# Layer 1 of a hybrid network: where D u is computed, which engine adds a scan's steps, and how fine the convolution is scheduled

## The chip, the cores and the metric

The kernel runs on one core of a Trainium2 chip. A core has five engines with a queue of instructions each, taken in order: TensorE (PE, matrix products into PSUM), VectorE (DVE), ScalarE (ACT), GpSimd (POOL) and SyncE (SP, which here starts the DMA transfers). They meet through semaphores. The metric is the device time of one execution in microseconds; before the change the median of three runs is 7093.66 us.

## What is computed

The input is 16 images of 96 channels, 56 x 56, in float32. Four layers follow each other; only the second, layer 1, is touched by the change. It is a block with a selective scan (cut from the reference):

```python
u = _ln(z, norm1_g, norm1_b) @ in_proj_w.T                  # 96 -> Din = 192
uc = silu(conv_general_dilated(uc, conv_w, 'SAME', feature_group_count=Din))   # 3x3, nine taps
xs = stack([xf, xt, xf[..., ::-1], xt[..., ::-1]], axis=1)  # four directions
dt = softplus(einsum('bkrl,kdr->bkdl', dts, dt_projs_w) + dt_projs_b)
a = exp(dt * A)                                             # N = 1
bb = dt * Bs * xs
h = associative_scan(comb, (a, bb))                         # h = a h + bb along l
y = h * Cs + Ds * xs                                        # per direction
ym = _ln(y summed over the four directions); z = z + ym @ out_proj_w.T
z = z + fc2(gelu(fc1(_ln(z))))                              # 96 -> 384 -> 96
```

(`dts`, `Bs` and `Cs` are projections of `xs`; the parts that only reshape are left out.) The term D u is the same for all directions up to order, so the kernel uses the sum of the four D.

## The kernel before

Layer 1 keeps the 192 channels as one tile of 128 rows (`u0`) and one that holds the last 64 twice, once straight and once turned (`um`). Six combinations of channels and direction (i = 0 to 5) times two halves of the image are 12 *units*, and a unit has two parts of 784 positions: 24 *steps* per image, counted from 0 in the order i = 0, 3, 1, 4, 2, 5 (four steps each). The steps of i = 1 and 4 read u with rows and columns exchanged (turned).

A step on its engines:
- PE: p_d, two products that make dt's argument (L1237), queued in one stream with everything else that PE does.
- ACT: dt by an exponential (L1244) and a logarithm (L1246), then a by an exponential (L1253). The two a of a unit come after both its dt.
- SP: the rows B and C for the step, spread over the partitions by a DMA (bc, L1266).
- DVE: dt times u (L1325), times B into PSUM (L1328), the scan (L1334 forward, L1336 backward); and, one step late, hc = scan times C (L1289).
- The sum over directions: y lies in a tile of the pool `big`. For i = 0 and 2 (steps 0 to 3 and 16 to 19) DVE writes y = D u + hc (L1292, a scalar_tensor_tensor). For the other 16 steps POOL adds hc to y (L1358). hc has one buffer. After the last step DVE folds the turned half of the 64 channels into the straight one with four additions (L1363).

Around the scans of one image stand two more pieces, of its neighbours. The *front* of the next image: norm sums (p_s), input projection p_in (L1130), convolution p_c (L1170) as nine taps, each a diagonal product, in six blocks of 36 products by `convolved`, copies out of PSUM on ACT (L1191), two Silus (L1193), projection p_x (L1207), its copy (L1209) and the store of proj for the bc rows (L1213). The *back* of the image before: variance of y by squares (L1379, L1381) and p_v (L1387), `vr` on ACT and DVE (L1052, L1054), a root on POOL (L1404), then seven groups: p_o (L1417, L1418, L1425), z on DVE (L1428, L1432), squares (L1438), the variance (L1440 to L1443), a root on POOL (L1445), the product zn (L1447), a transpose p_t (L1451) and its copy (L1454), p_f and gelu (L1461, L1463), p_g (L1471, L1472) and z (L1474). The groups run as three chains; zn has one buffer, z and xr two.

The order of all this is not written out by hand. Each piece is a Python generator that yields an `Op` (engine, cost in us, buffers taken and given back) before the instructions it stands for. `in_order` picks, at every turn, the waiting piece with the smallest planned start plus a *lead* (a bias by engine and generator, table `TUNED`), and so fixes the order of each engine's queue when the program is built. An Op is one block: nothing can be put between its instructions. `hold` is added to an ACT piece that needs another table set. The lines of the planner and of the pieces that change:

```python
if op.engine == "ACT" and op.table and op.table != tables.get("ACT"):
    start, key = max(ready, engines.get("ACT", 0.0) + change["ACT"]), key + hold
...
if best is None or (start + key, rank) < best[:2]:
    best = (start + key, rank, i, start)
```

Seven tiles `big` serve u0, um and the two y of up to three images; y of the 64 channels gets the tile of u0 once its last step has read it.

Of the kernel before, what the change touches and what calls it, by code (L numbers as in the profile page):

```python
# [23 lines left out]
T = 448  # L24
# [35 lines left out]
def packed(x):  # L60
# [96 lines left out]
    for m in (C, DIN):  # L157
# [22 lines left out]
                        'zn': 1,  # L180
# [3 lines left out]
            'leads': {('PE', 'spreads'): -2.2,  # L184
                      ('PE', 'steps'): -3.4,
                      ('SP', 'sums'): -1.2,
                      ('ACT', 'spreads'): -0.3,
                      ('DVE', 'additions'): -0.2,
                      ('ACT', 'hidden'): -0.7,
                      ('SP', 'norms'): 0.7,  # L190
                      ('POOL', 'fronts'): -4.6,
                      ('DVE', 'some'): -0.3,
                      ('POOL', 'norms'): 0.4,
                      ('PE', 'some'): -0.6,
                      ('ACT', 'sums'): 0.5,
                      ('SP', 'projected'): -1.4,
                      ('DVE', 'norms'): 0.1,
                      ('POOL', 'backs'): -0.6,
# [3 lines left out]
                      ('ACT', 'fronts'): -0.2,  # L202
                      ('PE', 'fronts'): -2.4,
                      ('DVE', 'spreads'): -0.8,
                      ('SP', 'rows_of'): 0.2},
            'hold': 0.7,
# [52 lines left out]
def turned(ap):  # L259
    return ap.rearrange("c (h w) -> c w h", w=S)  # L260
# [626 lines left out]
def layer1(ctx, tc, src, given, dst, flags=None, soft=False):  # L887
# [151 lines left out]
    def pe(n, each, take=("ps",), give=(), **k):  # L1039
        return Op("PE", 1.05 * n * each, 0.25, take, give, **k)  # L1040
# [56 lines left out]
    def front(b, it):  # L1097
# [60 lines left out]
        def convolved(j):  # L1158

            pad, u = (whole, halves)[j], us[j]  # L1160
            for c in range(0, (8, 4)[j], 2):
                yield Op("none", 0.0, 0.0, take=("ps",))
                p = pair("p_c")
                yield pe(9, 0.66, ())
                for k in range(9):
                    for b in range(2):
                        r0 = 7 * (c + b) + k // 3
                        for s in range(2):
                            to = (s ^ b) * 64
                            nc.tensor.matmul(  # L1170
                                p[to : to + 64, b, :TC], taps[64 * s : 64 * s + 64, j, k],
                                pad[64 * s : 64 * s + 64, r0 : r0 + 7, k % 3 : k % 3 + S],
                                start=k == 0, stop=k == 8,
                            )
                at = TC * c
                if j == 0:
                    outs = [
                        (u[:, at : at + TC], p[:, 0, :TC], TC),
                        (u[:64, at + TC : at + 2 * TC], p[64:, 1, :TC], TC),
                        (u[64:, at + TC : at + 2 * TC], p[:64, 1, :TC], TC),  # L1180
                    ]
                else:
                    outs = []
                    for s, b in ((0, 0), (0, 1), (1, 0), (1, 1)):
                        to, row = (s ^ b) * 64, HALF_S * s + 7 * (c + b)
                        own = p[to : to + 64, b, :TC]
                        outs.append((u[:64, S * row : S * row + TC], own, TC))
                        outs.append((turned(u[64:])[:, row : row + 7], own.rearrange("p (h w) -> p h w", w=S), 1.7 * TC))
# [12 lines left out]
        for b in range(2):  # L1201
            yield pe(3, 0.7, ("ps",) if b == 0 else ())
# [17 lines left out]
    def made_of(it):  # L1220
# [4 lines left out]
        def steps():  # L1225

            for unit in units:
                i, h = unit
                order = (0, 1) if i < 3 else (1, 0)
                for s in order:  # L1230
# [11 lines left out]
                    else:  # L1242
                        yield act(SUB, give=("ps",), table="exp")
                        nc.scalar.activation(flat, p[:, :, :TC], AF.Exp, bias=dtb[:, i : i + 1])  # L1244
                        yield act(SUB, table="exp")
# [4 lines left out]
                for s in order:  # L1250
                    give = ("proj",) if last and s == order[1] else ()
                    yield act(SUB, give=give, table="exp", post=times[unit, s])
# [21 lines left out]
    def scanned(it):  # L1274
# [4 lines left out]
        def scan():  # L1279
            y0, ym = None, None  # L1280
            before, late = None, None

            def finish(unit, s, a, t, end, out, own_u):
                i = unit[0]
                yield dve(
                    SUB, take=("hc",), give=("bc",) + (("a",) if end else ()), post=None if i in (0, 2) else added[unit, s]
                )
                made[unit]["hc", s] = hc = buf([P, SUB], "hc")
                nc.vector.tensor_tensor(hc, a, t[:, 1], ALU.mult)  # L1289
                if i in (0, 2):  # L1290
                    yield dve(SUB, give=("hc",), post=added[unit, s])
                    nc.vector.scalar_tensor_tensor(  # L1292
                        out, own_u, dsum[:, i // 2 : i // 2 + 1], hc, ALU.mult, ALU.add
                    )

            for unit in units:
# [4 lines left out]
                if unit in ((0, 0), (2, 0)):  # L1301
                    yield Op("none", 0.0, 0.0, take=("big",))
                    y = big.pop(0)
                    if mixed:
                        ym = y
                    else:
                        y0 = y
                    it["y"].append(y)
                y = ym if mixed else y0
                for s in ((1, 0) if back else (0, 1)):  # L1310
# [10 lines left out]
                    yield dve(SUB, 1.85e-3 if flip else 1.04e-3, wait=times[unit, s], give=("big",) if free else ())  # L1321
                    if free:
                        big.append(u)
                    dt, a = made[unit][s], made[unit]["a"][:, SUB * s : SUB * s + SUB]
                    nc.vector.tensor_tensor(as_own(dt), as_own(dt), own(u), ALU.mult)  # L1325
                    yield dve(SUB, wait=bct[unit, s], give=("dt",))
# [11 lines left out]
                    late = (unit, s, a, t, end, own(y), own(u))  # L1338
            yield from finish(*late)

        def sums():
            for unit in units:
                i, h = unit
                back = i >= 3
                if i in (0, 2):
                    continue
                for s in ((1, 0) if back else (0, 1)):
                    at = HALF * h + SUB * s
                    yield Op("none", 0.0, 0.0, wait=added[unit, s])
                    y, u = it["y"][i == 5], (um if i == 5 else u0)  # L1350
# [6 lines left out]
                    yield Op("POOL", 1.9, give=("hc",))  # L1357
# [6 lines left out]

        it["sums"] = sums()
        yield from scan()

    def back(b, it):
# [38 lines left out]
        def group(g):  # L1407
# [18 lines left out]
            yield dve(4 * C1, take=("z",))  # L1426
# [17 lines left out]
            yield Op("POOL", 1.4)  # L1444
# [13 lines left out]
            def hidden(j):  # L1458
# [3 lines left out]
                yield act(T, table="gelu", give=("ps",))  # L1462
# [23 lines left out]
    def item():  # L1486
# [3 lines left out]
            "times": lists(), "bcs": lists(), "bct": lists(), "added": lists(),  # L1490
# [473 lines left out]
```

## Time and profile before

| | us |
|---|---|
| median of three runs (lowest, highest) | 7093.66 (7093.59, 7100.32) |
| the profiled execution | 7093.59 |
| its span, first to last instruction | 7091.7 |
| layer 1 within it, about | 1,146 to 4,402 |
| first scan, last scan of layer 1 | 1293 to 4288 |
| busy PE / DVE / ACT / POOL over the span | 6092.5 / 5440.8 / 4521.6 / 1377.5 |
| TensorE clock granted, mean | 0.904 |

Busy times of an engine count overlapping instructions once. The three layers on either side of layer 1 are one program with it, but do not overlap it: its scans lie in slices 8 to 24 of the page's 40. An instruction is given with the line of the kernel that issued it; "[7.13 <-ACT a L1253]" means that its engine stood idle for 7.13 us before it and that the last semaphore it waited for came from that line. PE's ends are modelled.

The costliest groups of layer 1 on the page are, per instruction: L1325 1304 ns, L1328 1010, L1289 968, the scans 1825, the additions L1358 2064, L1244 912, L1246 946, L1253 937.

### The profile page before, as it was taken

The page shows a single profiled execution, that of the slowest core. Times are in us where ns is not written, and L with a number is a line of the kernel's source. Part 1 is how long each engine was busy: PE and PEld are TensorE (multiplying, and loading weights), DVE is VectorE, ACT ScalarE, POOL GpSimd, SP SyncE. Part 2 cuts the span into 40 slices and gives each one's busy share as a digit, 9 for nine tenths or more (in the row PEclk, how much of TensorE's full clock was granted, in tenths as well). Part 3 has the DMA queues.
Part 4 walks back from the last instruction along what each step waited for, and adds up shares of the span by engine and source line. Part 5 has one row for each costly group of instructions (what it writes and reads, how often), then busy time and mean ns, then how long its engine had stood idle before and what let it go on. Part 6 is the DMA issues. An engine that isn't in the chain of part 4 may idle for free. (4 is left out here: it accounts for less than half of the span.)

```text
span 7091.7 us, 113066 instructions
## 1 busy us (share of the span) xinstructions
PE 6092.5 (86%) x45643; PEld 4183.4 (59%) x45643; DVE 5440.8 (77%) x7075; ACT 4521.6 (64%) x5897; POOL 1377.5 (19%) x898
## 2 busy tenths in 40 slices
PE   7999997888888888888888866788999989999986
PEld 3444443345445455555544444787888888888875
DVE  6786884598888888888888894667777777777775
ACT  4454542677777777777777762455666666666664
POOL 0000000233332323233332231111111111111110
PEclk9999997788898898888888867899999999999997
DMA  1111111444444444444544342445555455555542
GB/s 38 32 38 34 38 33 52 132 143 134 131 137 132 136 133 138 130 138 135 140 131 126 110 128 64 97 107 123 130 116 128 111 130 119 123 134 118 120 105 62
DMA packets 508374, 763.72 MB, mean 108 GB/s; under 512 B 206337, under 2 KB 339137, under 8 KB 504530
## 3 DMA queue, kind: packets, MB, share of 16 engines
q1 hardware_dynamic: 506818, 753.53, 41.2%
q8 instruction: 363, 5.95, 0.4%
q0 software_dynamic: 1024, 2.85, 0.1%
q14 instruction: 169, 1.38, 0.1%
HBM read 563.65 MB, written 192.59 MB: 107 GB/s over the span
## 5 line engine op out<-in xcount | busy, mean ns | idle before, releaser
L1664 POOL TENSOR_TENSOR r<-v,nhalf 112x16 f32<-112x16 f32 (+1 forms) x128 | 392.9, 3076 | 2238.8 <-DVE v L1662 1677.2
L1358 POOL TENSOR_TENSOR big<-big,hc 128x784 f32<-128x784 f32 x256 | 528.3, 2064 | 1139.4 <-DVE hc L1289 1131.3
L1325 DVE TENSOR_TENSOR dt<-dt,big 128x784 f32<-128x784 f32 x384 | 500.6, 1304 | 249.4 <-ACT a L1253 249.1
L827 DVE SCALAR_TENSOR_TENSOR h<-pad,rows,h 128x1568 f32<-128x1568 f32 x288 | 525.9, 1844 | 3.9
L1244 ACT ACTIVATE dt<-p_d,l_dtb 128x784 f32<-128x784 f32 x384 | 350.3, 912 | 183.0 <-PE p_d L1237 157.8
L1237 PE MATMUL p_d<-proj,l_dt 32*128 32x392 f32 x1536 | 382.8, 581 | 93.5 <-ACT big L1191 52.4
L1461 PE MATMUL p_f<-zt,w_fc 96*128 96x448 f32 x672 | 401.7, 731 | 41.9 <-ACT zt L1454 27.8
L1471 PE MATMUL p_g<-l_fc,hid 128*112 128x96 f32 x2688 | 425.5, 304 | 11.7 <-ACT hid L1463 11.0
L1722 PE MATMUL p<-k_f,z 112*128 112x112 f32 x3072 | 375.0, 282 | 67.5 <-DMA z<-d 57.9
L1722 PEld LDWEIGHTS p<-k_f,z 112*128 112x128 f32 x3072 | 370.6, 199 | 76.3 <-issue 57.9
L1471 PEld LDWEIGHTS p_g<-l_fc,hid 128*112 128x112 f32 x2688 | 385.4, 219 | 41.0 <-ACT hid L1463 30.8
L1770 PE MATMUL p_v<-w,gg 128*112 128x97 f32 x2048 | 377.9, 267 | 34.5 <-DVE gg L1759 11.6
L1170 PE MATMUL p_c<-x,taps 64*64 64x392 f32 x4608 | 400.8, 497 | 0.8 <-ACT big L1191 0.8
L1328 DVE TENSOR_TENSOR drive<-dt,bc 128x784 f32<-128x784 f32 x384 | 387.8, 1010 | 10.2
L1771 PE MATMUL p_v<-w2both,gg 128*112 128x97 f32 x2048 | 376.0, 266 | 0.0
L1289 DVE TENSOR_TENSOR hc<-a,bc 128x784 f32<-128x784 f32 x384 | 371.8, 968 | 3.4 <-POOL big L1358 3.4
L1246 ACT ACTIVATE dt<-dt,one 128x784 f32<-128x784 f32 x384 | 363.4, 946 | 8.5
L1691 PE MATMUL p_a<-first,xt 97*112 97x192 f32 x1792 | 336.6, 336 | 18.1 <-ACT xt L1685 9.0
L1334 DVE TENSOR_TENSOR_SCAN a<-a,drive 128x784 f32<-128x784 f32 x192 | 350.3, 1825 | 0.0
L1336 DVE TENSOR_TENSOR_SCAN a<-a,drive 128x784 f32<-128x784 f32 x192 | 350.2, 1824 | 0.0
L1253 ACT ACTIVATE a<-dt,aneg 128x784 f32<-128x784 f32 x384 | 347.5, 937 | 2.7 <-DVE a L1334 1.4
L800 PE MATMUL p_c<-pad,taps 64*64 64x392 f32 x4032 | 347.4, 494 | 0.3 <-ACT pad L782 0.3
(341 smaller groups left out, 14838.7 us busy)
## 6 DMA issues: line engine op xcount, KB each, us to landing
bc<-bc SPq DMA_DIRECT2D x256, 784.0 KB
bc<-bc SPq DMA_DIRECT2D x256, 392.0 KB
d<-y SPq DMA_DIRECT2D x448, 192.0 KB
z<-d SPq DMA_DIRECT2D x128, 672.0 KB
d<-uu SPq DMA_DIRECT2D x256, 169.8 KB
z<-d SPq DMA_DIRECT2D x192, 194.0 KB
xc<-x SPq DMA_DIRECT2D x96, 336.0 KB
x<-in_x SPq DMA_DIRECT2D x16, 1176.0 KB
```

Source lines behind the costliest of these rows:

```text
L827: nc.vector.scalar_tensor_tensor(out, view, taps9[:, i : i + 1], out, ALU.mult, ALU.add)
L1170: nc.tensor.matmul(p[to : to + 64, b, :TC], taps[64 * s : 64 * s + 64, j, k], pad[64 * s : 64 * s + 64, r0 : r0 + 7, k % 3 : k % 3 + S], s ...
L1237: nc.tensor.matmul(p[:, b, :TC], wdt[on, i], proj[on, h], start=True, stop=True)
L1325: nc.vector.tensor_tensor(as_own(dt), as_own(dt), own(u), ALU.mult)
L1328: nc.vector.tensor_tensor(b, dt, t[:, 0], ALU.mult)
L1358: nc.gpsimd.tensor_tensor(out, out, hc, ALU.add)
L1461: nc.tensor.matmul(p[:, 0, :T], w_fc1[:, P * j : P * j + P], zt, start=True, stop=True)
L1471: nc.tensor.matmul(p[:Q, q, :C], hid[:, j, own], fc2[:, j], start=j == 0, stop=False)
L1664: nc.gpsimd.tensor_tensor(r, v, nhalf[:, :n], ALU.pow)
L1722: nc.tensor.matmul(p[:, q, :Q], flat[:, P * (3 * q + k) : P * (3 * q + k) + P], f2, start=True, stop=True)
L1770: nc.tensor.matmul(out, gs[2 * h][:, at + k], w["w2"][:, 2 * h], start=True, stop=False)
L1771: nc.tensor.matmul(out, gs[1][:, at + k], w["w2both"][:, h], start=False, stop=True)
```

## The change

Layer 1 alone is changed, in four ways.

- y begins as D u. A new generator `inits`, beside the scan, lets ACT write y = (sum of D) times u, for each half of both tiles: four instructions of 1568 positions per image. The scalar_tensor_tensor on DVE is gone, and POOL adds hc in all 24 steps. A count `uses` frees u0 and um when both the scan and `inits` have read them.
- The nine taps of a convolution block are three Ops of three taps (12 products) in place of one of nine.
- zn has two buffers.
- Costs, leads and `hold` of the planner have other values, and some leads are new or gone.

```diff
@@ TUNED
-                        'zn': 1,
+                        'zn': 2,
-            'leads': {('PE', 'spreads'): -2.2,
+            'leads': {('PE', 'spreads'): -0.9,
-                      ('SP', 'sums'): -1.2,
+                      ('SP', 'sums'): 1.2,
-                      ('POOL', 'fronts'): -4.6,
+                      ('POOL', 'fronts'): -6.6,
-                      ('DVE', 'norms'): 0.1,
-                      ('POOL', 'backs'): -0.6,
+                      ('DVE', 'norms'): 1.5,
-                      ('PE', 'fronts'): -2.4,
+                      ('SP', 'some'): 4.2,
+                      ('ACT', 'inits'): 0.7,
+                      ('PE', 'hidden'): -1.2,
...
-            'hold': 0.7,
+            'hold': 0.0,
@@ estimates
-        return Op("PE", 1.05 * n * each, 0.25, take, give, **k)
+        return Op("PE", 1.1 * n * each, 0.25, take, give, **k)
...
@@ convolved
-                yield pe(9, 0.66, ())
                 for k in range(9):
+                    if k % 3 == 0:
+                        yield pe(3, 0.66, ())
                     for b in range(2):
@@ scan
-            def finish(unit, s, a, t, end, out, own_u):
+            def finish(unit, s, a, t, end):
...
                 nc.vector.tensor_tensor(hc, a, t[:, 1], ALU.mult)
-                if i in (0, 2):
-                    yield dve(SUB, give=("hc",), post=added[unit, s])
-                    nc.vector.scalar_tensor_tensor(
-                        out, own_u, dsum[:, i // 2 : i // 2 + 1], hc, ALU.mult, ALU.add
-                    )
...
+                    if free:
+                        it["uses"][mixed] -= 1
+                        if it["uses"][mixed] == 0:
+                            big.append(u)
+                            yield Op("none", 0.0, 0.0, give=("big",))
@@ sums
-                if i in (0, 2):
-                    continue
...
+                    yield Op("none", 0.0, 0.0, wait=it["begins"][i in (2, 5), h])
-                    yield Op("POOL", 1.9, give=("hc",))
+                    yield Op("POOL", 2.1, give=("hc",))
                     nc.gpsimd.tensor_tensor(out, out, hc, ALU.add)
@@ new
+        def inits():
+            for j, u in enumerate((u0, um)):
+                if j:
+                    yield Op("none", 0.0, 0.0, wait=added[(4, 1), 1])
+                yield Op("none", 0.0, 0.0, take=("big",))
+                y = big.pop(0)
+                it["y"].append(y)
+                for h in range(2):
+                    yield act(HALF, post=it["begins"][j, h])
+                    cols = slice(HALF * h, HALF * h + HALF)
+                    nc.scalar.activation(y[:, cols], u[:, cols], AF.Identity, scale=dsum[:, j : j + 1])
+                it["uses"][j] -= 1
+                if it["uses"][j] == 0:
+                    big.append(u)
+                    yield Op("none", 0.0, 0.0, give=("big",))
+
         it["sums"] = sums()
-        yield from scan()
+        yield [scan(), inits()]
```

## The prediction

> **What bounds the kernel now.** I read the slices of the page first: they show three stages, and only layer 1 (about 1,146 to 4,402 us) is touched. Then I read the busy times in windows over one image of its steady part, from the end of one image's four L1363 additions (2404.4) to the end of the next (2594.6), then the waits by engine, then the timeline at the longest waits. Columns of the windows: length; busy us (and count) of PE, weight loads, DVE, ACT, POOL; granted TensorE clock, DMA share, GB/s.
>
> ```profile
> 2404.40:2594.60 190.20, 163.64 (x1261) 93.93 (x1257) 163.00 (x179) 145.96 (x184) 58.78 (x40) 0.88 0.47 135
> ...
> 2424.20:2454.60 30.40, 23.96 (x281) 10.89 (x277) 20.34 (x22) 27.38 (x34) 5.33 (x3) 0.94 0.32 111
> 2454.60:2484.00 29.40, 23.97 (x159) 12.08 (x158) 18.47 (x27) 19.10 (x26) 14.40 (x16) 0.73 0.45 141
> 2484.00:2594.60 110.60, 99.00 (x631) 63.56 (x629) 105.30 (x114) 82.83 (x101) 39.05 (x22) 0.90 0.53 144
> ```
>
> A step is one of an image's 24 scans, counted from 0. An image takes 190.2 us; PE and DVE are busy 164 and 163 of them, so neither is the bound alone. The two middle rows (steps 4 to 7, and 8 with most of 9) hold 10.1 + 10.9 = 21.0 of DVE's 27.2 idle us; in the last row DVE is busy 95%. So the image has two regimes: while the next image's convolution runs, DVE waits; in the rest DVE is the bound. DVE's first row of waits (releaser; us in total, times, longest; 1,400 to 4,200 us) says for what, and the timeline (start, us, engine, line) shows an image's two longest, each as PE's queue and then DVE's step:
>
> ```profile
> DVE dt L1325 <- ACT a L1253: 223.3, 50, 10.8
> ```
> ```profile
> 2418.95 6.84 PE L1170 MATMUL p_c<-half,taps 64*64 64x392 f32 x72
> 2425.72 0.93 PE L1237 MATMUL p_d<-proj,l_dt 32*128 32x392 f32 x4
> ```
> ```profile
> 2431.45 0.97 DVE L1325 TENSOR_TENSOR dt<-dt,big 128x784 f32<-128x784 f32 x1 [7.13 <-ACT a L1253]
> ```
> ```profile
> 2454.47 6.69 PE L1207 MATMUL p_x<-big,l_xw 128*32 128x392 f32 x48 [2.62 <-ACT big L1193]
> 2461.09 0.93 PE L1237 MATMUL p_d<-proj,l_dt 32*128 32x392 f32 x4
> ```
> ```profile
> 2464.83 1.65 DVE L1325 TENSOR_TENSOR dt<-dt,big 128x784 f32<-128x784 f32 x1 [8.91 <-ACT a L1253]
> ```
>
> Both have one form: the small p_d matmul that feeds the next exponentials stands in PE's queue behind a block of 6.8 us (a whole nine-tap convolution, then the whole projection p_x), and DVE's step waits for the chain p_d, dt, a behind it.
>
> [...] the zn product L1447 takes 0.55 us alone and 2.57 under a GpSimd addition:
>
> ```profile
> 2314.81 2.57 DVE L1447 TENSOR_TENSOR zn<-z,r 112x384 f32<-112x384 f32 x1 [0.41 <-POOL r L1445]
> ...
> 2322.73 0.55 DVE L1447 TENSOR_TENSOR zn<-z,r 112x384 f32<-112x384 f32 x1
> ```
> ```profile
> 2314.74 2.23 POOL L1358 TENSOR_TENSOR big<-big,hc 128x784 f32<-128x784 f32 x1
> ```
>
> The scan [...] keeps 1.8 us beside additions. [...] the trace agrees (3136 elements 2.82, 784 elements 0.94: 0.80 ns), so D u over 1568 costs 0.94 + 784 x 0.80 ns = 1.57 us. [...] in the built order of layer 1 the loads are 242 before and 244 after.
>
> **The change part by part,** per image, by the order of instructions of both builds and the durations above.
> (1) The eight L1292 leave DVE. From hc to the scan it is 2366.26 to 2368.22 with one, 2390.35 to 2391.23 without: 1.96 - 0.89 = 1.07 each, 8.6 us. Four stand in steps 1 to 4, before a wait, four in steps 17 to 20, where DVE is the bound.
> (2) ACT gains 4 x 1.57 = 6.3 us (146 to 152 of the span). One stands among the exponentials of steps 0 and 1, one ahead of those of steps 2 and 3, two in a row (3.1 us) before those of step 18; queued behind these is a of step 18, which L1325 waits for. ACT may run ahead of DVE by three steps (three dt), so I take 1.5 us lost here (bounds 0 and 3.1). The second pair waits for a free big, which is u0 after step 15; ACT gets there later than that, cost 0.
> (3) POOL gains 8 additions of 1.85 us (a straight L1358; 2.23 is a turned one): 59 to 74 us. Each starts with the scan, which it doesn't block, and ends some 0.1 us into the next L1325 (1.08 against 0.97): 0.8 us. hc has one buffer; the next hc comes 4.5 us later at least, so the wait is 0 except after the 4.81 us root L1404, which now stands just ahead of step 4's addition: up to 0.9, under another wait.
> (4) zn products behind hc: before, by starts and ends in the trace, 59 of 112 ran into an addition, 3.7 per image at 1.92 against 0.55, 1.37 more; in the new order two per image stand right behind hc (steps 12, 21), 3.6 in all against 5.1: gain 1.5. The four L1363 now come right behind the last hc, not two instructions later, and wait about 2 us for its addition, against 1.54 that L1328 lost before (2.52 at 2395.28 against 0.98): loss 0.5. (3) and (4) cancel.
> (5) Taps in blocks of 12 matmuls (2.05 us). The built PE order uses it: 12 taps between three p_v groups, 24 then a p_v group, 12 before p_d. Steps 2 to 9 followed by hand on the three queues: p_d of step 4 still has three p_v groups and 36 taps ahead (about 11 us), yet p_d of step 3 comes earlier, and the wait at step 4 falls from 7.1 (6.0 on average) to 1 to 3. Gain 4.
> (6) p_x moves behind p_d of step 9 (before, it stood ahead of it), so a of step 8 needs the two Silus, not p_x. Chain: table 1.28 + Silus 5.64 + two squares 1.05 + variance 0.33 + table 1.28 + dt 1.85 + a 0.93 = 12.4 us, of which DVE fills about 8 with the second zn group (zn has two buffers now). The wait of 8.9 (with others in step 8: 10.0) becomes 3 to 5. p_x then lies under steps 8 and 9. Gain 5.5.
> (7) New lumps: between a of step 1 and a of step 2 ACT has some 18 us (four p_v preparations, nine copies, D u), which steps 0 and 1 with L1363 cover to about 1 us; step 20's exponentials follow two rounds of gelu and come 2 to 3 us late. Loss 2 more.
> SP: the built order has ten bc loads before the four proj stores (nine before), and proj is stored under step 9; bc of step 10 is then in time: 0. The other edits (estimates, hold, leads) act only through this order.
> Sum: 8.6 - 1.5 + 4 + 5.5 - 2 = 14.6, an image of about 175.6 us. There DVE would be busy 153 to 154, idle 22. My hand-followed queues close at 173; the difference is what such a count leaves out.
> Thirteen images run at the full pitch (L1363 comes every 188 to 191 us; its first and last intervals are 180 and 176, one is 194): 13 x 14.6 = 190. The first two and the last lack a back or a front: about 8.6 each, 26. The tail of the last back, where zn had one buffer: 0 to 5, taken 2. In all 218. The profiled span is 7091.7, its run 7093.59, 0.07 from the median: 7093.6 - 218 = **6876 us**.
>
> **Rivals.** (A) The waits only move: DVE's idle 27 us per image stays and just the 8.6 of DVE work goes. For: PE is busy 164 and has as much work as before. Against: 21 us of idle hang on two named blocks. 13 x 8.6 + 26 = 138: 6956. (B) Convolution steps gain nothing (PE is the bound there, four of the L1292 lie before a wait), only 4.3 in steps 17 to 20: 13 x 4.3 + 15 = 71: 7023. (C) More: fewer gaps also raise the granted clock (0.73 in the row of the p_x wait, 0.94 before it), p_d and gelu matmuls shorten, the pitch is 170: 13 x 20 + 30 = 290: 6804. (D) Slower: ACT becomes the bound through its order. The 18 us between a of steps 1 and 2 is not covered if p_v, one ysq buffer at a time, waits for PE's tap blocks: each of four rounds then costs about 2 us more, 8; the 3.1 of D u at step 18 and 3.4 at step 20 show fully, 2 at L1363: 16.5 of new waits against 8.6 gained, and (5) and (6) do not come: 13 x 8 = 104, about 7198. It decides when new waits pass 18 us per image. Against: ACT is busy 77% and ahead by up to three steps.
>
> **How the numbers follow.** Likeliest 0.50 (6820 to 6930), A 0.19, B 0.08, C 0.15, D 0.06, and 0.02 for no net effect. Pitches of 168 to 185 give 6780 to 7010; below lies a third of C (0.05), above D and part of B (0.11). 0.2% is 14 us, about what a measurement tells from no change. Faster 0.92, within 0.02, slower 0.06.
>
> **What would show it.** Right: pitch of L1363 near 176 us; L1325's wait for a down from 223 to about 100 in layer 1; DVE busy near 154 per image; no p_x between p_d and a of steps 8 and 9; POOL near 1,377 + 128 x 1.85 = 1,614 us. Wrong: ACT waits in L1325 at steps 2, 18 or 20 of over 4 us each; additions waiting for D u; hc waiting for POOL over 1 us per image; zn products near 2.5 us more often than now.

## The result, and the profile after

The changed kernel takes 7056.81 us (median of five runs, 7036.49 to 7063.0), the kernel before 7100.32 in the same session (7093.59 to 7112.2). The ratio is 0.9934, 95% interval 0.9915 to 0.9953: about 44 us faster, where 218 were forecast; 7056.8 lies 47 us above the upper end of the range. Layer 1 itself became 46.6 us shorter (it ends at 4355.6 us of the span, before at 4402.2). The untouched layers behind it took 9 us longer in this one profile, so its span fell by only 37.5, to 7054.2.

The same cut of the trace as before, windows over one image of the steady part: the whole image from the last L1352 (the old L1363) to the next, then its convolution steps (about 1 to 10), then the rest. Columns as in the prediction: length; busy us (and count) of PE, weight loads, DVE, ACT, POOL; granted TensorE clock, DMA share, GB/s. The changed kernel, then the same two parts of an image in the kernel before:

```profile
2397.78:2585.47 187.69, 166.82 (x1265) 94.70 (x1263) 152.56 (x170) 151.68 (x188) 73.16 (x48) 0.87 0.47 137
2397.78:2481.38 83.60, 74.72 (x750) 37.83 (x749) 60.39 (x69) 75.13 (x98) 27.85 (x23) 0.94 0.36 118
2481.38:2585.47 104.09, 92.10 (x517) 56.87 (x516) 92.17 (x103) 76.55 (x91) 45.31 (x26) 0.82 0.56 152
```
```profile
2404.44:2491.00 86.56, 71.61 (x670) 36.16 (x666) 63.30 (x70) 68.71 (x89) 21.11 (x20) 0.84 0.35 113
2491.00:2594.87 103.87, 92.27 (x594) 57.97 (x594) 99.94 (x110) 77.24 (x95) 37.67 (x21) 0.92 0.56 152
```

DVE is busy 152.6 us per image, as forecast (153 to 154). But the image takes 187.7 us and not 176: DVE now stands idle for 35.1 of it, before for 27.2. What left DVE came back as waiting. In the convolution steps ACT and PE are now busy for 90% of the time (75.1 and 74.7 of 83.6; before 79 and 83%), DVE for 72%. The rest of the image is no shorter than before (104.1 us against 103.9), although DVE has 7.8 us less to do in it: its idle time there rose from 3.9 to 11.9 us.

What DVE waits for, in the waits by engine (releaser; us in total, times, longest; 1,400 to 4,200 us). The changed kernel, then two lines of the kernel before:

```profile
DVE z L1479 <- PE p_g L1477: 156.5, 62, 6.0
DVE dt L1310 <- ACT a L1257: 128.2, 58, 4.7
DVE vr L1057 <- ACT vr L1055: 98.3, 51, 4.0
DVE big L1352 <- POOL big L1347: 27.4, 14, 2.0
```
```profile
DVE z L1474 <- PE p_g L1472: 74.1, 50, 3.8
DVE vr L1054 <- ACT vr L1052: 35.6, 52, 3.3
```

The wait for a (223.3 before) fell to 128.2, where about 100 was forecast, and no single one reaches 5 us. But z behind the gelu products rose from 74.1 to 156.5, vr from 35.6 to 98.3, and the first of the four L1352 of an image waits 2.0 us for GpSimd's last addition.

By step (busy and idle time between the ends of successive scans, my mean over the fourth to the fourteenth image of each trace), DVE's idle time moved as follows:

| step | 0 | 2 | 4 | 6 | 8 | 10 | 18 | 19 | 20 | all 24 |
|---|---|---|---|---|---|---|---|---|---|---|
| before | 0.7 | 0.5 | 6.0 | 1.1 | 10.0 | 1.6 | 2.6 | 0.1 | 0.1 | 27.4 |
| after | 4.5 | 7.2 | 4.7 | 4.5 | 3.2 | 2.9 | 0.0 | 2.1 | 2.3 | 35.6 |

By what ended it, the new idle time of step 0 is 2.3 us for p_g and 2.0 at the first L1352, that of step 6 is for vr and a, that of steps 19 and 20 for p_g.

Step 2 has the largest wait of the changed kernel. Its timeline (start, us, engine, line; in brackets the idle time ahead) shows DVE's queue and ACT's beside it:

```profile
2408.18 0.36 DVE L1057 SCALAR_TENSOR_TENSOR vr<-vr,p_v 128x196 f32<-128x196 f32 x1 [1.69 <-ACT vr L1055]
2412.57 0.36 DVE L1057 SCALAR_TENSOR_TENSOR vr<-vr,p_v 128x196 f32<-128x196 f32 x1 [4.03 <-ACT vr L1055]
2414.80 0.97 DVE L1310 TENSOR_TENSOR dt<-dt,big 128x784 f32<-128x784 f32 x1 [1.88 <-ACT a L1257]
```
```profile
2409.43 0.95 ACT L1250 ACTIVATE dt<-dt,one 128x784 f32<-128x784 f32 x1
2410.41 0.89 ACT L1195 COPY big<-p_c 64x392 f32<-64x392 f32 x1
2411.32 0.86 ACT L1384 ACTIVATE ysq<-big 128x784 f32<-128x784 f32 x1
2412.20 0.33 ACT L1055 ACTIVATE vr<-p_v 128x196 f32<-128x196 f32 x1
2412.56 0.85 ACT L1386 ACTIVATE big<-big 64x784 f32<-64x784 f32 x1
2413.44 0.48 ACT L1195 COPY big<-p_c 64x392 f32<-64x392 f32 x1
2413.82 0.95 ACT L1257 ACTIVATE a<-dt,aneg 128x784 f32<-128x784 f32 x1
```

Between the logarithm of dt and the a that uses it, ACT runs copies and a round of squares without a gap, 3.4 us of it; DVE meanwhile stands before vr, and then before a. D u is no part of this: its last instruction ahead of step 2 ends at 2395.96, and ACT then waits 1.88 us for p_d. Step 4 then waits 4.65 us, for another reason: its a is made once both p_d of its unit are done. On PE the first of them comes 14 us behind the p_d ahead of it, with three p_v rounds, taps and norm sums in between, and the second, on which ACT waits for 4.1 us, after three more blocks of three taps (x24 each, since the trace has two records for each product):

```profile
2403.30 0.93 PE L1241 MATMUL p_d<-proj,l_dt 32*128 32x392 f32 x4
...
2418.23 0.93 PE L1241 MATMUL p_d<-proj,l_dt 32*128 32x392 f32 x4 [0.53 <-ACT big L1195]
2419.72 2.21 PE L1174 MATMUL p_c<-half,taps 64*64 64x392 f32 x24 [0.56 <-ACT big L1195]
2421.74 2.16 PE L1174 MATMUL p_c<-x,taps 64*64 64x392 f32 x24
2423.72 2.16 PE L1174 MATMUL p_c<-half,taps 64*64 64x392 f32 x24
2425.81 0.93 PE L1241 MATMUL p_d<-proj,l_dt 32*128 32x392 f32 x4
```

Of the 46.6 us of layer 1, the eleven intervals in the middle (190.46 on average before, 188.22 after) give 25, the last three (558.7 before, 526.1 after) 32.6; the stretch from the last L1352 to the end of the layer gives 8.7 back, the start about 2.

### The profile page after: what moved, and what is told of

Read it like the earlier page. It is cut to its first block, busy times and chain, and to the rows that moved or that the text cites. A ratio compares the mean times of both kernels' runs of the same rounds, so it can differ in the third digit from the quotient of the medians.

```text
span 7054.2 us, 113146 instructions
## 1 busy us (share of the span) xinstructions
PE 6135.4 (87%) x45643; PEld 4203.5 (60%) x45643; DVE 5268.4 (75%) x6947; ACT 4618.1 (65%) x5963; POOL 1598.2 (23%) x1026
## 5 line engine op out<-in xcount | busy, mean ns | idle before, releaser
L1347 POOL TENSOR_TENSOR big<-big,hc 128x784 f32<-128x784 f32 x384 | 764.2, 1990 | 1539.5 <-DVE hc L1290 1493.0
L1174 PE MATMUL p_c<-x,taps 64*64 64x392 f32 x4608 | 429.9, 504 | 1.6 <-ACT big L1195 1.4
L1775 PE MATMUL p_v<-w,gg 128*112 128x97 f32 x2048 | 378.5, 267 | 33.5 <-DVE gg L1764 11.4
L1466 PE MATMUL p_f<-zt,w_fc 96*128 96x448 f32 x672 | 364.2, 687 | 22.3 <-ACT zt L1459 15.6
```

What stands on the lines that cost most here:

```text
L1174: nc.tensor.matmul(p[to : to + 64, b, :TC], taps[64 * s : 64 * s + 64, j, k], pad[64 * s : 64 * s + 64, r0 : r0 + 7, k % 3 : k % 3 + S], s ...
L1347: nc.gpsimd.tensor_tensor(out, out, hc, ALU.add)
L1775: nc.tensor.matmul(out, gs[2 * h][:, at + k], w["w2"][:, 2 * h], start=True, stop=False)
```

## The experiments

Times are medians; "ratio" is that to the kernel before in the same session, with its 95% interval. "Pitch" is the mean of eleven middle intervals of the image sums (L1363 or its successor) in the profiled run: 190.5 before, 188.2 after.

### 1. What one engine's work is worth, the order held fixed

My first theory on seeing the two traces was Q: PE's queue, busy for 90% of the convolution steps, is what they now wait for. Its rival V is the prediction's own accounting, in which DVE ends each step. The first cuts take away DVE's eight multiply-adds, about the same amount of DVE work in the changed kernel, and two thirds of the taps in both. The edits, with nothing else moved, are below; stt16_before, and later ln16_stt16_before and du16_after, also fill the big tiles once ahead of the first scan (18.6 us on POOL), so for these three the pitch says more than the time:

```diff
-  out, own_u, dsum[:, i // 2 : i // 2 + 1], hc, ALU.mult, ALU.add
+  out[:, :16], own_u[:, :16], dsum[:, i // 2 : i // 2 + 1], hc[:, :16], ALU.mult, ALU.add
```
```diff
+  n = 16 if i in (0, 2) else None
-  nc.vector.tensor_tensor(as_own(dt), as_own(dt), own(u), ALU.mult)
+  nc.vector.tensor_tensor(as_own(dt)[:, :n], as_own(dt)[:, :n], own(u)[:, :n], ALU.mult)
```
```diff
   for s in range(2):
+      if k % 4:
+          continue
```

> The kernel before with the eight multiply-adds of an image (L1292) cut to 16 of their 784 columns, so most of y in these steps is left out; its order of work is untouched, only a fill of the seven big tiles ahead of layer 1 is new (once, under 30 us). VectorE loses about 8 x 0.9 = 7.2 us per image. Theory Q (the chain through the scans runs over TensorE and ScalarE for more than half of the time, and these eight stand on it for only some 2.2 of their 8.6 us per image): pitch of the image sums 190.3 to 187.5-189.5, time 10 to 40 us less. Rival V (term 1 of the prediction: VectorE ends every step, its time counts in full): pitch 183 to 184, time about 90 to 105 us less.

> The changed kernel with the multiplication of dt by u (L1310) cut to 16 of 784 columns in the eight scans of an image over directions 0 and 2, so most of that product is left out; order untouched. VectorE loses about 8 x 0.85 = 6.8 us per image, as much as the change took from it. Theory Q (TensorE's queue is what the convolution steps wait for): pitch 187.7 to 185.5-187.7, time 0 to 35 us less. Rival V (VectorE still ends each step and the gain was lost to a worse order): pitch 181 to 182, time 80 to 100 us less.

> The kernel before with three of the nine convolution taps issued, so two thirds of layer 1's depthwise convolution are left out; order untouched. TensorE loses about 25 us per image in the steps 0 to 10. Theory Q: TensorE is on the chain there, but less than in the changed kernel: pitch 190.3 to 180-186, time 60 to 150 us less. Rival V: VectorE ends each step, only its waits for p_d's followers at steps 4 and 8 (16 us per image) can go: also 174 to 186; the two kernels gain alike.

> The changed kernel with three of the nine convolution taps issued, so two thirds of layer 1's depthwise convolution are left out; order untouched. TensorE loses about 25 us per image in the steps 0 to 10, where it is busy for some 95 per cent of the time. Theory Q (TensorE's queue is the bound in these steps): pitch 187.7 to 165-176, time 160 to 300 us less, clearly more than in the kernel before, and VectorE's waits at steps 0 to 8 fall from 24 us per image below 12. Rival V (the new order and estimates cost the gain, TensorE has slack): pitch 180 or more, no more gain than in the kernel before.

| run | us | ratio | pitch |
|---|---|---|---|
| stt16_before | 7090.8 | 0.9996 (0.9987 to 1.0006) | 190.5 |
| dtu16_after, a single run | 7044.6 | | 188.5 |
| taps3_before, a single run | 7035.9 | | 187.7 |
| taps3_after, a single run | 7005.3 | | 186.5 |

Six us less on DVE per image (156.9 busy instead of 162.9), and neither time nor pitch moves; in the changed kernel the 12 us are inside what single runs scatter (7036 to 7063). Rival V is refuted, but so is theory Q: PE's busy time fell by 20 and 14 us per image (164 to 145, 166 to 152), and 2.8 and 1.7 came of it, no more in the changed kernel than before (on this point V was right). The waits by engine of stt16_before show DVE's time turned into waiting (its lines stand two further down):

```profile
DVE dt L1327 <- ACT a L1255: 243.1, 53, 10.7
DVE z L1476 <- PE p_g L1474: 99.3, 65, 5.6
DVE vr L1056 <- ACT vr L1054: 64.8, 69, 3.3
```

Against 223.3, 74.1 and 35.6 before, that is 74 us more in the window's 14.7 images, 5 each: most of the six.

The next four ask whether ACT's queue holds the steps (theory S); its rival L says that several queues hold one another, so that relief of any one returns little. The cuts are of the in-place logarithm in steps 0 to 11, with and without the cut of L1292, and of D u:

```diff
-  nc.scalar.activation(dt, dt, AF.Ln, bias=one)
+  n = 16 if i in (0, 3, 1) else SUB
+  nc.scalar.activation(dt[:, :n], dt[:, :n], AF.Ln, bias=one)
```
```diff
-  cols = slice(HALF * h, HALF * h + HALF)
+  cols = slice(HALF * h, HALF * h + 16)
```

> The kernel before with the in-place logarithm of dt (L1246) cut to 16 of 784 columns in the scans of directions 0, 3 and 1 (steps 0 to 11), so dt is left wrong by that logarithm there; order untouched. ScalarE loses about 12 x 0.75 = 9 us per image, all in the convolution steps. Theory S, formed after the cut of L1292 gave nothing: ScalarE's queue (convolution evictions, dt, a) is what steps 1 to 10 end with, since it is busy for 42.4 of the 46.6 us of steps 1 to 7: pitch 190.3 to 183-186.5, time 50 to 110 us less. Rival L (several queues in fixed order hold one another, none alone sets a step; any one relief returns less than a quarter): pitch 188 to 190, time 0 to 35 us less.

> The kernel before with both cuts: the logarithm of dt (L1246) on 16 columns in steps 0 to 11 and the multiply-add of D u (L1292) on 16 columns, so dt's logarithm and most of y are left out there; the fill of the big tiles ahead of layer 1 is in it (under 30 us, once). Theory S: with ScalarE relieved VectorE's time begins to count, the two together give clearly more than the logarithm alone, 3 to 6 us per image on top: pitch 178 to 183. Rival L: the two add up to what each gave alone, pitch 188 to 190.

> The changed kernel with the in-place logarithm of dt (L1250) cut to 16 of 784 columns in steps 0 to 11, so dt is left wrong by that logarithm there; order untouched. ScalarE loses about 9 us per image in the convolution steps, where it now also makes D u. Theory S: steps 2, 8 and 10 end with ScalarE (busy for 12.4 of 12.7, 12.5 of 13.4 and 9.2 of 9.5 us): pitch 187.7 to 179-184, time 60 to 130 us under the changed kernel's 7056.8. Rival L: pitch 185.5 to 187.5, at most 35 us less.

> The changed kernel with D u (L1364) on 16 of 1568 columns, so y begins from old contents of its tile and D u is left out; order untouched, and a fill of the big tiles ahead of layer 1 is new (once, under 30 us). ScalarE loses 4 x 1.45 = 5.8 us per image, half of it in steps 0 to 2. Theory S (the new work on ScalarE took the place of what left VectorE): pitch 187.7 to 183-185.5, time 35 to 70 us under the changed kernel's. Rival L: pitch 186.5 to 187.7, 0 to 20 us less.

| run | us | ratio | pitch |
|---|---|---|---|
| ln16_before | 7071.2 | 0.9959 (0.9943 to 0.9974) | 188.4 |
| ln16_stt16_before | 7026.9 | 0.9892 (0.9838 to 0.9946) | 185.0 |
| ln16_after | 7015.0 | 0.9875 (0.9842 to 0.9908) | 185.3 |
| du16_after | 7052.9 | 0.9942 (0.9913 to 0.9971) | 188.1 |

Theory S falls too, and L is nearer but not right either: 7.5 us of ACT per image (145.7 to 138.3 and 151.5 to 143.9 busy) return 2 to 3, and D u on ACT costs nothing that can be seen (0.9942 without it, 0.9934 with it). But together the two cuts of before return 5.5 us per image, where one by one they gave 0.0 and 2.1 and L has them add up; and ln16_after gives 42 us, where L allows 35. So L1292 seems to be worth something only where ACT has been relieved as well; the double cut has two runs, 26 us apart. The last cut joins three in the changed kernel:

> The changed kernel with all three cuts that were made one by one: dt times u on 16 columns in directions 0 and 2, the logarithm of dt on 16 columns in steps 0 to 11, three of nine taps; these parts are left out, order untouched. VectorE loses 6.8, ScalarE 9 and TensorE 25 us per image. Theory K (the steps are held by several queues at once, so cuts pay together): one by one they gave 12, 42 and 52 us; together 150 to 260 us less than the changed kernel. Rival: they add up, 90 to 120 us less, or less than the largest two, since something else (a transfer, a buffer) bounds the steps: under 80.

It took 6927.4 us (0.9763, 0.9743 to 0.9782), 129 less than the changed kernel, where the three gave 12, 42 and 52, in all 106; pitch 181.1. That lies between the two expectations: the cuts seem to help one another, but by less than theory K said. Two of the three are single runs, so 23 us are not much; in pitch the three gave 4.4 one by one and 7.1 together. With 28 us less busy time on three engines (DVE 152 to 145, ACT 152 to 144, PE 166 to 152) an image is only 7 us shorter.

### 2. The parts of the change, each planned anew

Here the change was taken apart at its own seams, with the planner free to make a new order: D u alone (L1364, all 24 additions on POOL, nine taps in one Op, old estimates and leads); the three blocks alone; the new estimates, leads and zn 2 alone; and the change with one nine-tap Op.

```diff
-  yield pe(9, 0.66, ())
   for k in range(9):
+      if k % 3 == 0:
+          yield pe(3, 0.66, ())
```

(this is three_alone; after_nine undoes the same lines in the changed kernel.)

> The kernel before with D u alone: y begins on ScalarE, GpSimd adds all 24, no L1292; nine taps in one block, the estimates, leads and buffers of before. Theory L (fixed queues that hold one another; relief of one engine returns under a quarter, and D u on ScalarE costs as little): 0 to 25 us less than before. Prediction's terms 1 to 3 (8.6 gained, 1.5 lost per image): about 100 us less.

> The kernel before with the taps in three blocks alone: L1292 stays, and the estimates, leads and buffers of before. Theory L: within 20 us of before, either way. Prediction's term 5 (the waits for a at step 4 fall from 6 us to 1 to 3): 40 to 60 us less, and VectorE's idle time in step 4 falls from 6.0 us below 3.

> The kernel before with the new estimates, leads and zn 2 alone: L1292 stays on VectorE and the nine taps stay one block. Theory L: the plan brings the larger part of the change's 40 us, since no engine's load matters by itself: 15 to 50 us less than before. Rival: the new plan was fit to the lighter VectorE and without that it loses: 10 to 60 us more than before. Prediction's term 6 would show as VectorE's idle time in step 8 falling from 10 us to 3 to 5.

> The changed kernel with the nine taps in one block again, all else of the change kept. Theory L: within 20 us of the changed kernel's 7056.8. Prediction's term 5: 40 to 60 us more, about 7100 to 7115.

| run | us | ratio | eleven middle intervals, lowest to highest |
|---|---|---|---|
| du_alone | 7256.5 | 1.0228 (1.0194 to 1.0261) | 183.5 to 230.8 |
| three_alone | 7202.0 | 1.0162 (1.0141 to 1.0184) | 178.6 to 215.1 |
| estimates_alone | 7527.3 | 1.0618 (1.0598 to 1.0638) | 168.2 to 307.2 |
| after_nine | 7415.2 | 1.0460 (1.0441 to 1.0480) | 184.8 to 240.6 |

Every expectation is missed, by up to ten times its size. Each part alone loses 110 to 440 us, and the change without its three blocks 360, though none adds that much work: estimates_alone has the very same work as the kernel before. What is lost is the regular order. The kernels before and after repeat one order from image to image (188.4 to 191.2 and 187.7 to 189.8); these four do not. Windows over two neighbouring images of estimates_alone, columns as above:

```profile
2977.79:3235.93 258.14, 209.30 (x1695) 116.00 (x1687) 161.64 (x183) 183.38 (x231) 59.24 (x40) 0.84 0.39 109
3235.93:3408.92 172.99, 131.72 (x770) 71.14 (x771) 151.51 (x156) 104.22 (x132) 54.38 (x37) 0.71 0.45 128
```

One image's scans carry 209 us of PE and 183 of ACT work, the next one's 132 and 104: the fronts have slipped, so that DVE waits in one image and runs ahead in the next. These runs do not price the parts; they price a plan whose leads were not set for its list of pieces.

### 3. Work and order crossed

So the order was held, and only the instructions at given places of it exchanged: the change's work in the order of before, and the work of before in the changed kernel's order. In the first, with `before`'s planner untouched:

```diff
-  nc.vector.scalar_tensor_tensor(
-      out, own_u, dsum[:, i // 2 : i // 2 + 1], hc, ALU.mult, ALU.add
-  )
+  nc.gpsimd.tensor_tensor(out, out, hc, ALU.add)
...
   it["y"].append(y)
+  for n in range(2):
+      cols = slice(HALF * n, HALF * n + HALF)
+      nc.scalar.activation(y[:, cols], u[:, cols], AF.Identity, scale=dsum[:, i // 2 : i // 2 + 1])
```

> The plan of before, unchanged, but at the places of the eight L1292 the instruction issued is GpSimd's addition of hc to y, and D u is issued on ScalarE where y is taken (ahead of steps 0 and 16): the change's work in the order of before; the whole of the reference is computed. Theory O (the order decides, the work moved weighs little): within 25 us of before, either way, pitch 188.5 to 192. Rival W (the work that left VectorE is the gain, and the new order gave most of it back): 60 to 110 us less than before, pitch 182 to 186.

> The plan of the changed kernel, unchanged, but D u is not issued on ScalarE and at the places of the eight additions of directions 0 and 2 VectorE issues the multiply-add of D u and hc (the old L1292) in place of GpSimd's addition: the work of before in the changed kernel's order; the whole of the reference is computed. Theory O: within 25 us of the changed kernel's 7056.8, so 10 to 60 us faster than before, though no work left VectorE. Rival W: VectorE's 8.6 us per image come back in full, 90 to 120 us over the changed kernel, so 50 to 90 us slower than before.

| | order of before | order of after |
|---|---|---|
| work of before | 1 (pitch 190.5) | 0.9976 (0.9963 to 0.9988), 7086.8 us, pitch 190.4 |
| work of after | 1.0056 (1.0042 to 1.0070), 7139.2 us, pitch 193.3 | 0.9934 (0.9915 to 0.9953), 7056.8 us, pitch 188.2 |

Neither pure theory holds. The new order alone is worth some 17 us; in the profiled run its steady pitch is that of before, and the gain lies in the last three intervals (531.6 us against 558.7). The new work alone costs some 40 us in the old order, and is worth some 30 in the new one. Where the old order punishes it, two halves of it show:

> The plan of before, unchanged, with the change's work for direction 0 alone (D u on ScalarE ahead of step 0, four additions on GpSimd in place of four L1292); direction 2 stays on VectorE. The whole of the reference is computed. Reading M of the run with both (its steps 0 to 15 were 0.6 us, its steps 16 to 23 2.2 us longer than before): direction 0 costs nothing, 0 to 15 us over before, pitch about 190.5 to 191.5. Rival: both halves lose alike, 15 to 30 us over before.

> The plan of before, unchanged, with the change's work for directions 2 (mixed) alone (D u on ScalarE ahead of step 16, four additions on GpSimd in place of four L1292); direction 0 stays on VectorE. The whole of the reference is computed. Reading M: the loss is here, at step 16 (behind D u on ScalarE) and at step 20 (zn of L1447 beside GpSimd's additions): 25 to 40 us over before, step 20 longer by 2.5 to 3.5 us. Rival: 10 to 20 us.

Direction 0 alone: 7100.9 us, ratio 1.0007 (0.9995 to 1.0019), pitch 190.6. Direction 2 alone: 7140.9, ratio 1.0066 (1.0049 to 1.0083), pitch 193.8. Reading M holds for the place, and the loss is somewhat larger than its 25 to 40 us: 47, all of it in direction 2. In new_work_old_order steps 16 and 17 are 1.1 and 0.5 us longer than before, 18 and 19 are 1.1 and 1.0 shorter, and step 20 is 3.0 longer, 11.4 us instead of 8.3. The timeline of step 20 in the kernel before, and in new_work_old_order (lines shifted by one):

```profile
2563.79 1.59 POOL L1445 TENSOR_TENSOR r<-v,nhalf 112x4 f32<-112x4 f32 x1 [12.66 <-DVE v L1443]
...
2564.56 1.03 DVE L1292 SCALAR_TENSOR_TENSOR big<-big,dsum,hc 128x784 f32<-128x784 f32 x1
...
2565.51 0.55 DVE L1447 TENSOR_TENSOR zn<-z,r 112x384 f32<-112x384 f32 x1
```
```profile
2582.79 1.67 POOL L1446 TENSOR_TENSOR r<-v,nhalf 112x4 f32<-112x4 f32 x1 [5.50 <-DVE v L1444]
2584.43 1.84 POOL L1292 TENSOR_TENSOR big<-big,hc 128x784 f32<-128x784 f32 x1
2584.50 2.19 DVE L1448 TENSOR_TENSOR zn<-z,r 112x384 f32<-112x384 f32 x1 [0.91 <-POOL r L1446]
2586.61 1.77 DVE L1335 TENSOR_TENSOR_SCAN a<-a,drive 128x784 f32<-128x784 f32 x1
```

Before, L1292 filled the time that GpSimd needs for the root r, and zn then ran in 0.55 us. With L1292 gone DVE waits 0.91 us for r, and zn starts beside the addition that took its place and lasts 2.19: 1.03 us less work, and 0.91 + 1.64 = 2.55 more time. The rest of step 20's loss is a wait of 1.33 us for p_g, which DVE reaches earlier now that steps 18 and 19 are shorter. Over all zn products (1,400 to 4,150 us) the mean rose from 1,317 to 1,769 ns, for seven of them 3.2 us per image.

### 4. The granted clock

Nothing so far said why cutting the taps returns so little. In taps3_after the taps that stay became slower, in taps3_before they hardly did. Groups by line, 1,400 to 4,150 us (count; busy us, mean ns of one; idle ahead), the changed kernel, taps3_after, then the kernel before and taps3_before:

```profile
L1174 PE MATMUL p_c<-x,taps 64*64 64x392 f32 x4032 | 375.1, 502 | 1.6 <-ACT big L1195 1.4 <-DVE v L1407 0.3
```
```profile
L1176 PE MATMUL p_c<-x,taps 64*64 64x392 f32 x1344 | 196.5, 666 | 6.1 <-ACT big L1197 3.1 <-DVE v L1409 2.9
```
```profile
L1170 PE MATMUL p_c<-x,taps 64*64 64x392 f32 x4032 | 346.7, 493 | 0.8 <-ACT big L1191 0.8
L1172 PE MATMUL p_c<-x,taps 64*64 64x392 f32 x1344 | 125.1, 502 | 0.1
```

So slower taps explain part of it in the changed kernel only. In the kernel before PE's busy time did fall by 20 us per image, and its pitch by 2.8.

The clock records show two levels, full and half speed, and change between them on a grid of 3.413 us: of the 334 records of the kernel before and the 326 of the changed kernel all but the last of each are whole multiples of it long. Six of these stretches of the changed kernel, around a fall and the next rise (columns as above, the granted clock third from the end):

```profile
2551.84:2555.25 3.41, 3.41 (x22) 2.26 (x22) 3.38 (x5) 1.96 (x3) 2.69 (x3) 1.00 0.17 64
2555.25:2558.67 3.42, 1.46 (x6) 0.30 (x4) 3.35 (x8) 3.01 (x5) 1.17 (x1) 1.00 1.09 240
2558.67:2562.08 3.41, 3.19 (x8) 1.77 (x8) 3.41 (x5) 2.57 (x4) 2.61 (x2) 0.50 0.57 166
...
2568.91:2572.32 3.41, 3.41 (x19) 3.21 (x18) 2.20 (x2) 3.37 (x4) 1.85 (x1) 0.50 0.54 203
2572.32:2575.73 3.41, 3.41 (x21) 3.14 (x24) 0.29 (x1) 0.63 (x1) 0.00 (x0) 0.50 0.11 37
2575.73:2579.15 3.42, 3.42 (x36) 1.23 (x32) 1.47 (x3) 0.54 (x1) 1.83 (x1) 1.00 0.36 100
```

In the changed kernel 28% of the stretches ran at half speed (1,400 to 4,150 us, mean granted clock 0.86; 26% before, at 0.87; 37, 40 and 41% in taps3_before, taps3_after and three_cuts_after, at 0.81, 0.80 and 0.79). There the clock fell after a stretch with TensorE busy for between 0.12 and 0.64 of it (half of the cases under 0.46), and rose only after one above 0.8. Of its stretches at full speed all 55 with TensorE busy for less than half were followed by one at half speed, of those between 0.5 and 0.7 it was 30 of 59, and above 0.7 none of 465. In the kernel before it was 63 of 67, 23 of 65 and 7 of 461, the highest at 0.72. What sets the clock no run isolated. One run fills the waits of TensorE that recur in every image:

```diff
+  def busy(p, n):
+      for _ in range(n):
+          nc.tensor.matmul(p[:C, 0, :192], ident[:C, :C], w_fc1[:, :192], start=True, stop=True)
...
   p = pair("p_t")
+  busy(p, {2: 4, 4: 1}.get(g, 0))
```

> The changed kernel with 13 matmuls of 192 columns more per image, whose results are overwritten, ahead of six matmuls that wait once per image (p_r 1.58 us, p_s of the fourth part 2.01, p_in of the fourth part 2.19, the twelfth p_d 1.43, p_t of groups 2 and 4 3.3 and 1.2); the whole of the reference is computed. Observation: the granted clock changes between 1 and 1/2 on a fixed grid of 3.413 us, and falls after a stretch of that length in which TensorE was busy less than about 55 to 70 per cent; 28 per cent of the stretches of layer 1 are at half speed in the changed kernel, and 37 with three of nine taps. Theory W (the waits of TensorE cost twice, as a gap and as slow stretches behind it): share at half speed from 0.28 to under 0.18, TensorE busy under 158 us per image although it has more to do, pitch 178 to 186, time 25 to 130 us under the changed kernel's 7056.8. Rival: the added matmuls delay what stands behind them as much as the clock gains, or the slow stretches stay: 20 us less to 40 us more.

It took 7071.6 us, ratio 0.9960 (0.9944 to 0.9975): no better than the changed kernel. In the profiled run, the slowest of six, the share at half speed fell only from 0.28 to 0.26 (its mean granted clock over the whole span is 0.902, that of the changed kernel 0.900), and pitch rose to 190.9. The rival holds for this dose. Whether another filling would keep the clock up was not tried.

## Why the prediction was wrong

The direction was right, and most of the single durations; the sum was wrong by five times. By its own steps:

(1) "The eight L1292 leave DVE", 8.6 us: they left (DVE busy 163.0 to 152.6 in the windows, with the effects of (4) among it), but the term was entered as time. At a fixed order it measured 0.0 (stt16_before), and moved to ACT and POOL it measured 2.2 (190.4 to 188.2) in the order of after and -2.8 in that of before. The sentence "four in steps 17 to 20, where DVE is the bound" is where this went wrong: DVE was busy 95% there, yet without them steps 18 and 20 just stood idle longer (2.6 to 3.4 and 0.1 to 1.8 us in stt16_before). Busy is not bound.

(2) and (3), D u and POOL: the durations were right. D u takes 1.587 us (1.57 forecast), and of the 244 table loads of layer 1 (242 before; 1.28 us each) none is at its line; its removal changes the pitch by 0.2; hc waits for POOL 4.2 us in fourteen images; POOL is busy 1,598 (1,614). The 1.5 us charged to step 18 did not come: its idle time fell from 2.6 to 0.0.

(4) Beside GpSimd's additions: L1352's wait of 2.0 us came as said. zn fell from 1,317 to 734 ns on average, 4.0 us per image instead of 1.5, in DVE's busy time. In the changed kernel the ten zn products that start under an addition take 2,371 ns, the 87 that meet none 554; why, no run shows.

(5) Step 4: its wait should fall from 6.0 to between 1 and 3; it is 4.65, one third of the gain. The lump of three p_v rounds and 36 taps stands ahead of its p_d as forecast, but takes 14 us and not about 11, with norm sums and waits in it; and its a needs the second p_d of the unit too, another 36 taps later, which its text does not name.

(6) Step 8: its idle time fell from 10.0 to 3.2, p_x gone from before p_d. Right, 6.8 instead of 5.5.

(7) "New lumps", loss 2: this is the term that failed. Outside steps 4 and 8, DVE's idle time grew from 11.4 to 27.8 us, by 16.4. The largest, at step 2, has the place and in the main the cause that the prediction named, four p_v rounds and copies on ACT, but it said that steps 0 and 1 cover them "to about 1 us"; step 2 stands idle for 7.2 (0.5 before). D u, which it counted among them, costs nothing there: with D u cut (du16_after) step 2 is idle for 7.25. Step 20 waits 2.1, as long as forecast, but for p_g and not for the exponentials. Steps 0, 6 and 19, with 3.8, 3.4 and 2.0 more, were not on the list, apart from the 2.0 at L1352. The sum in measured terms: 10.9 less busy, 1.3 and 6.8 less waiting at steps 4 and 8, 16.4 more waiting elsewhere: 2.6 per image, against 14.6. The crossing divides this. In old_work_new_order, counted alike, DVE is busy 4.1 us less than before and waits 2.3 and 6.8 less at steps 4 and 8, but 12.9 more elsewhere: nothing is left, so the new order's own waits ate its gain. The work then taken from DVE, 6.9 us of its busy time, brings 4.5 of waiting with it, and 2.4 remain.

The hand count followed queues for steps 2 to 9 from the state that before had at step 2, and never closed them over a whole image. The nearest time was rival B's 7023, but not for its reason, since step 8 did gain. Rival A (the waits only move, DVE's idle time stays at 27) was the right kind of answer and still too kind: idle time grew to 35. Rival D's four rounds of 2 us did come, 7.2 of them, though not for its reason: ACT ran from 2397.84 to 2422.66 without a gap, so that the rounds stood in ACT's own queue and did not wait for PE's taps; D's other waits were not as large. The waits named as signs of being wrong did not come: in the eleven images of the table no wait for a at steps 2, 18 and 20 is over 1.9 us. The part of the gain that nobody forecast is in the last three intervals, 32.6 of 46.6 us (9.8, 13.7 and 9.1). The convolution of a next image runs through the first of them, into the second, and not in the third, so its absence does not explain them; their cause is open.

That the gain hangs on order and work together is supported by the crossing, and the slip of the untuned plans by their intervals. Not settled is how the image's length comes about from several queues and the clock; no run isolated that.

## What to carry over

When three engines are each busy for 75 to 90% in one fixed order, price a saving by the cut of just that work at an unchanged order, not by its duration; here 6 us of 163 were worth nothing, and 28 us on three engines 7. Before trusting a forecast of waits, follow every queue over one whole period until it ends where it began. An edit to a list that a tuned greedy planner orders is a new plan: compare by exchanging instructions at fixed places, since the parts planned anew say more about the leads than about the parts.

## Of the hardware

Beside the clock's grid and the half-busy stretches above, one thing was not expected. The distance between image sums is often close to a whole multiple of the clock's grid: 187.7, 191.1, 184.3 and 180.9 us are 55, 56, 54 and 53 times 3.413. Of the 176 middle intervals of the sixteen kernels with a regular order, 73 lie within 0.2 us of a multiple, where 21 would by chance (0.4 / 3.413), and of the 22 of the kernels before and after 14; but the intervals of one kernel repeat one another, so these are fewer than 176 independent cases. taps3_before has 187.4 to 187.9 in all eleven, with a third of the taps, and the changed kernel 187.7 to 187.9 in eight. This would explain in part why different cuts end at the same pitch; it was observed and not tested.
